# A fused attention, feed-forward and gating layer: normalized tokens transposed by VectorE and through DRAM in place of TensorE

## The chip, the cores and the metric

The kernel runs on one core of one Trainium2 chip. The time is that of the device in microseconds, from the first to the last instruction of one execution; three runs of the kernel before were timed. The profile is of one execution of its own.

## What is computed

x is [8, 2048, 512] in fp32: 8 batches of 2048 tokens. Cut to what matters:

```python
xn = layernorm(x)                          # over the 512 channels
q = xn @ Wq.T + bq                         # 8 heads of 8 channels
k = xn @ Wk.T + bk                         # 8 heads of 8 channels
v = xn @ Wv.T + bv                         # 8 heads of 64 channels
scores = leaky_relu(q k^T / sqrt(8), 0.2)  # 2048 x 2048 for each head and batch
s = gamma * (softmax(scores) @ v) + xn
g = silu(xn @ W.T + gated low-rank experts(xn))   # gate: softmax over 4, top 1
out = x + s * g
```

## The kernel before

**Tiles and stages.** A batch is cut into NB = 4 blocks of 512 tokens (BLK), a block into NT = 4 tiles of 128 tokens; the channels are NC = 4 groups of 128. Attention runs over 16 stripes in each batch: a stripe s is one pair of heads (NPAIR = 4) and one block of 512 queries. A stripe has CH = 16 steps, one for each 128 keys. The main loop runs over all 8 x 16 stripes and 16 steps of each, 2048 steps. In each step TensorE makes the scores of the next step for two heads (`score`, L641), one unit of the row maxima of a later stripe (`max_unit`, L586), and subtracts the maxima from this step's scores (`less_max`, L658); ScalarE does the leaky ReLU (`leaky`, L652) and the exponential (`exp`, L670); VectorE reduces the maxima (L597); GpSimd adds up the exponentials (`add_up`, L702). TensorE's products with the values (`weigh`, L682, "a value pair" for one step's two heads) wait in a list `last` until they are taken out one or two steps at a time.

**Work beside the attention.** Between these, `half_full` in each step issues a piece of background work from Python generators: `ending` (normalizes and stores a finished stripe), `shift_rows` (prepares a stripe's maxima and sends them through DRAM: L623 and L630) and `back`, the list of tasks. For each batch b the tasks are, in this order: `lift_block` 1 and 2 (gate and feed-forward of a block of batch b), `project_block` 0 and 1 of batch b + 1 (query, key and value projections), `lift_block` 3, `project_block` 2 and 3, and `lift_block` 0 of batch b + 1. Their due times come from estimated costs (A1 for a projection, A2 for a lift) spread over stripes 1.3 to 13.8 of the batch (`due_at`); a task may run ahead by AHEAD = 6 units. `spend` counts what was done. A generator's yield tells what comes next: HOLD (in the midst of matmuls into one PSUM bank), WAIT (the next piece waits for another engine), TINY (a short piece of TensorE), FREE, SLOW, IDLE. `half_full` has four branches:

```python
if go_on():                      # a generator in WAIT went on
    values(run); return
if state[j] == TINY:             # one value pair and the short piece
    values(min(run, 1)); go(j); ended[0] = True
elif len(last) > MUCH - (state[j] != HOLD) or (ended[0] and run > 1):
    for g in stats.values(): next(g, None)   # one piece of norm
    values(run)                  # value pairs
else:
    go(j); ...                   # matmuls of a task, two if in HOLD
```

**The place of the change.** While the task before a `project_block` runs, `norm` of its block is advanced in the third branch: statistics of four tiles on VectorE (L304, L305), their power on GpSimd, the first tile's normalization on ScalarE (L319, from tile xt into tile xn). `project_block` runs what is left of `norm`, then transposes each 128-token tile by four TensorE matmuls with the identity (L370, into PSUM tile tp), normalizes the next one meanwhile, and copies the result on VectorE (L373) to xnT, which holds channels on partitions and 512 tokens in the free dimension. Then it loads x for the block after the next (`load_x`, L111), projects queries and keys (`project`, L265, rhs xnT), splits them (`split_keys`, eight stores to KS and QS, L338 and L343), stores xn to XN (L389) and xnT to XT (L390) in DRAM, and projects the values (`token_major`, L279, lhsT xnT). `lift_block` reads xnT back from XT (`fetch`, L328). All DMAs are issued by SyncE's queue (SP), in program order; an issue that has to wait holds up those behind it. `load_stacks` (L542 k, L548 q_sb) loads a stripe's keys and queries at the start of the second stripe before it; the maxima of that stripe begin six steps later. Batch 0 is normalized and transposed ahead of the loop by code of its own (`turn`, L932), with nothing to hide it.

A token's place: a block's token p * 4 + t lies on partition p in tile t (`(n p t)`). Attention sums over all keys, so any order serves as long as queries, outputs, x and XN agree.

Of the kernel before, what the change touches and what calls it, by code (L numbers as in the profile page):

```python
# [20 lines left out]
BLK = 512  # L21
# [11 lines left out]
def fused_layer_kernel(  # L33
# [44 lines left out]
    xv = x.rearrange("b (n p t) c -> b n p t c", p=128, t=NT)  # L78
    ov = out.rearrange("b (n p t) c -> b n p t c", p=128, t=NT)
# [18 lines left out]
    XN = [tc.dram_tile([NB, 128, NT, C], FP, name=f"XN{b}") for b in range(B)]  # L98
    XT = [tc.dram_tile([NB, 128, NC, BLK], FP, name=f"XT{b}") for b in range(B)]

# [4 lines left out]
    def load_x(b, n):  # L105
        xt = two.tile([128, NT, C], FP, name="xt")
        if (b, n) == (0, 0):
            for t in range(NT):
                nc.sync.dma_start(out=xt[:, t, :], in_=xv[b, n][:, t, :])
        else:  # L110
            nc.sync.dma_start(out=xt, in_=xv[b, n])  # L111
        xtiles[b, n] = xt
# [136 lines left out]
    def spend(cost):  # L249
        spent[0] += cost  # L250
# [8 lines left out]

    def project(ps, wt, xnT):  # L260
        for c in range(NC):
            for part in pieces():
                if c or part.start:
                    yield HOLD
                nc.tensor.matmul(  # L265
                    ps[:, part],
                    lhsT=wt[:, c, :],
                    rhs=xnT[c][:, part],
                    start=(c == 0 and part.start == 0),
                    stop=(c == NC - 1 and part.stop == BLK),  # L270
                )
                spend(MM / len(pieces()))

    def token_major(ps, wt, xnT, t, more=False):
        for c in range(NC):
            for part in pieces():
                if c or part.start:
# [3 lines left out]
                    lhsT=xnT[c][:, t * 128 : (t + 1) * 128],  # L281
# [6 lines left out]
    def columns(*tiles):  # L288
        return [a[:, c, :] for a in tiles for c in range(a.shape[1])]
# [8 lines left out]
    def norm(b, n):  # L298
# [17 lines left out]
        xn = two.tile([128, NT, C], FP, name="xn")  # L316

        def normalize(t):
            nc.scalar.activation(  # L319
                xn[:, t, :], xt[:, t, :], AF.Identity, bias=nmr[:, t : t + 1], scale=rstd[:, t : t + 1]  # L320
            )

        normalize(0)
        normed[b, n] = xn, normalize
# [36 lines left out]
    def project_block(b, n, prefetch):  # L361
# [3 lines left out]
        xn, normalize = normed.pop((b, n))  # L365
        xnT = two.tile([128, NC, BLK], FP, name="xnT")
        for t in range(NT):
            tp = bank([128, NC, 128], "tp")
            for c in range(NC):
                nc.tensor.transpose(tp[:, c, :], xn[:, t, c * 128 : (c + 1) * 128], ident)  # L370
            if t + 1 < NT:
                normalize(t + 1)
            nc.vector.tensor_copy(xnT[:, :, t * 128 : (t + 1) * 128], tp)  # L373
            spend(0.5)
            yield TINY if t + 1 < NT else FREE
        if prefetch:
            fetch(*prefetch)
        nxt = b * NB + n + 2
        if nxt < B * NB:
            load_x(nxt // NB, nxt % NB)  # L380

        ps = bank([128, BLK], "qkps")
        yield from project(ps, wqk_sb, columns(xnT))
# [5 lines left out]
        nc.sync.dma_start(out=XN[b][n], in_=xn)  # L389
        nc.sync.dma_start(out=XT[b][n], in_=xnT)  # L390
# [5 lines left out]
        for t in range(NT):  # L396
            ps = bank([128, C], "vps")
            yield from token_major(ps, wv_sb, columns(xnT), t)
# [6 lines left out]
    def lift_block(b, n, prefetch, cols=None):  # L405
# [3 lines left out]
        if not early:  # L409
            if (b, n) not in fetched:  # L410
                fetch(b, n)
            cols = columns(fetched.pop((b, n)))
# [293 lines left out]
    def read_for_ending(s):  # L706
# [9 lines left out]
        nc.sync.dma_start(out=xs[:, 1], in_=XN[b][n][:, :, cols])  # L716
# [49 lines left out]
    A1, A2, LIFTED, KEYED, VALUED = 20 * MM + 2.0, 24 * MM + 3.7, 1.3, 13.8, 15.0  # L766
# [79 lines left out]

    def half_full():
# [8 lines left out]
        if go_on():  # L856
            values(run)
            return
# [3 lines left out]
        if j is not None and state[j] == TINY:  # L862
            values(min(run, 1))
            go(j)
            ended[0] = True
        elif j is None or len(last) > MUCH - (state[j] != HOLD) or (ended[0] and run > 1):
            ended[0] = False
            for g in stats.values():
                next(g, None)
# [32 lines left out]
    with tc.manual_schedule():  # L902
# [5 lines left out]
        def normalize_all(own, n):  # L908
# [5 lines left out]
            nc.sync.dma_start(out=XN[0][n], in_=xn)  # L914
# [208 lines left out]
```

## Time and profile before

| | us |
|---|---|
| median of three runs | 5573.27 (5553.82 to 5576.89) |
| span of the profiled execution | 5580.8, 78283 instructions |
| TensorE (PE) busy | 5338.6, 96% |
| GpSimd (POOL) busy | 4778.5, 86% |
| ScalarE (ACT) busy | 4448.0, 80% |
| VectorE (DVE) busy | 3672.4, 66% |
| mean granted TensorE clock | 0.970 |
| DMA | 615.39 MB, 35.1% of 16 engines on SP's queue |

The profiled execution's own time is its span, from its first to its last instruction; nothing else is told of it. Busy is the time in which an engine works on an instruction; matmuls are pipelined and their ends modelled, so a busy TensorE is not at its peak. PEld is TensorE's weight load, which runs beside the matmuls. An fp32 matmul shows as two rows. A name such as `tp<-ident,xn` is the tile written and the tiles read, L370 the line of the kernel. What stands behind `<-` after a time is what ended the wait; a wait for several events is put down to the last. The granted clock is the share of full rate at which TensorE ran.

### The profile page before, as it was taken

The numbers are of one execution on the slowest core, as the hardware profiler recorded it, in microseconds if no ns is written. First come the engines' busy times: TensorE is split into PE (matmuls) and PEld (weight loads), VectorE is DVE, ScalarE is ACT, GpSimd is POOL, SyncE is SP. The second block draws the span as 40 slices with busy tenths as digits, with TensorE's granted clock in tenths as the row PEclk, the third lists the DMA queues.
The fourth block names the chain that finished last, engine by engine and source line by source line (L and its number), as shares of the span: only waits on it lengthen the run. The fifth ranks groups of instructions, "written<-read, shape, count | busy, mean of one in ns | idle before, by whom it ended". The sixth has DMA issues, their size and how long they took to land.

```text
span 5580.8 us, 78283 instructions
## 1 busy us (share of the span) xinstructions
PE 5338.6 (96%) x26258; PEld 1975.0 (35%) x26258; DVE 3672.4 (66%) x4990; ACT 4448.0 (80%) x8627; POOL 4778.5 (86%) x2906
## 2 busy tenths in 40 slices
PE   7999999999999999999999999999999999999998
PEld 3333333333333333333333333333333333333332
DVE  5665766667666666667667666676666667666663
ACT  1787888788887788878888788887788878888887
POOL 1887898889897889988899888898889988899898
PEclk9998999999998999999999999999999999999998
DMA  5333343334423343333432334323343242432221
GB/s 191 113 111 114 109 133 97 101 116 120 125 94 95 124 127 111 98 101 124 136 108 88 108 116 152 101 80 117 111 146 95 83 144 88 142 96 84 72 78 61
DMA packets 528265, 615.39 MB, mean 110 GB/s; under 512 B 44092, under 2 KB 438332, under 8 KB 491768
## 3 DMA queue, kind: packets, MB, share of 16 engines
q1 hardware_dynamic: 527864, 610.39, 35.1%
q8 instruction: 209, 3.42, 0.3%
q14 instruction: 192, 1.57, 0.1%
HBM read 407.88 MB, written 202.38 MB: 109 GB/s over the span
## 4 chain that ended last, share of the span: by engine, by line
PE 84%; ACT 8%; DMA 3%; DVE 2%; issue 1%; SPq 1%; POOL 0%; ACTq 0%; POOLq 0%; DVEq 0%
PE av L682 30%; PE sc L658 17%; PE zps L279 9%; PE vps L279 8%; PE mx L586 8%; ACT ex L670 5%; ACT sc L652 3%; DMA q_sb<-QS 2%; PE qkps L265 2%; PE pps L265 2%; PE dps L265 2%; PE atp L754 1%; PE dps L737 1%; PE tp L370 1%; DVE mxr L597 1%
## 5 line engine op out<-in xcount | busy, mean ns | idle before, releaser
L702 POOL TENSOR_TENSOR acc<-acc,ex 128x1024 f32<-128x1024 f32 x1792 | 4231.4, 2361 | 255.3 <-ACT ex L670 138.4
L597 DVE TENSOR_REDUCE mxr<-mx 128x2 f32<-128x1024 f32 x2030 | 2480.0, 1222 | 1209.7 <-PE sc L658 942.8
L670 ACT ACTIVATE ex<-sc 128x512 f32<-128x512 f32 x4096 | 2228.5, 596 | 951.8 <-PE sc L658 831.3
L652 ACT ACTIVATE sc<-sc 128x512 f32<-128x512 f32 x4096 | 2234.4, 591 | 17.9 <-PE sc L641 17.9
L682 PE MATMUL av<-ex,v_sb 128*64 128x512 f32 x8192 | 2140.3, 627 | 4.5 <-DVE avs L724 3.1
L658 PE MATMUL sc<-shift,ones_r 2*128 2x512 f32 x4096 | 1654.7, 462 | 77.7 <-ACT sc L652 65.8
L586 PE MATMUL mx<-k,q_sb 32*128 32x512 f32 x4096 | 1463.2, 453 | 66.3 <-DMA q_sb<-QS 62.4
L658 PEld LDWEIGHTS sc<-shift,ones_r 2*128 2x128 f32 x4096 | 694.8, 187 | 1542.3 <-ACT sc L652 1453.1
L641 PE MATMUL sc<-q_sb,k 32*128 32x512 f32 x4096 | 1036.4, 502 | 0.0
L682 PEld LDWEIGHTS av<-ex,v_sb 128*64 128x64 f32 x8192 | 468.6, 138 | 843.1 <-issue 819.5
L586 PEld LDWEIGHTS mx<-k,q_sb 32*128 32x128 f32 x4096 | 572.6, 187 | 90.5 <-issue 69.8
L279 PE MATMUL zps<-w_sb,xnT 128*128 128x512 f32 (+1 forms) x1120 | 529.0, 589 | 7.5 <-DMA xnT<-XT 7.5
L279 PE MATMUL vps<-wv_sb,xnT 128*128 128x512 f32 x960 | 477.1, 621 | 0.2
L702 POOL TENSOR_TENSOR acc<-ex 128x1024 f32<-128x1024 f32 x128 | 301.8, 2357 | 169.0 <-ACT ex L670 168.7
L641 PEld LDWEIGHTS sc<-q_sb,k 32*128 32x128 f32 x4096 | 385.4, 185 | 0.8 <-issue 0.8
L279 PEld LDWEIGHTS zps<-w_sb,xnT 128*128 128x128 f32 x1120 | 187.0, 190 | 234.9 <-issue 229.7
L279 PEld LDWEIGHTS vps<-wv_sb,xnT 128*128 128x128 f32 x960 | 164.5, 190 | 200.1 <-issue 198.7
L518 DVE SCALAR_TENSOR_TENSOR g<-th,zps 128x512 f32<-128x512 f32 x128 | 88.0, 688 | 185.0 <-ACT th L517 185.0
L611 POOL TENSOR_TENSOR ml<-m,big 128x8 f32<-128x8 f32 x128 | 26.2, 205 | 202.5 <-DVE m L610 196.3
L349 DVE TENSOR_TENSOR vb<-vps,bv_sb 128x512 f32<-128x512 f32 x120 | 82.9, 691 | 93.4 <-PE vps L279 93.2
L373 DVE COPY xnT<-tp 128x512 f32<-128x512 f32 x112 | 77.3, 690 | 97.5 <-PE tp L370 97.5
L265 PE MATMUL dps<-xnT,wd_sb 128*128 128x512 f32 (+1 forms) x280 | 134.4, 592 | 0.0
(124 smaller groups left out, 2717.7 us busy)
## 6 DMA issues: line engine op xcount, KB each, us to landing
v_sb<-VS SPq DMA_DIRECT2D x127, 1024.0 KB
k<-KS SPq DMA_DIRECT2D x256, 256.0 KB
XN<-xn SPq DMA_DIRECT2D x32, 1024.0 KB
q_sb<-QS SPq DMA_DIRECT2D x256, 128.0 KB
xnT<-XT SPq DMA_DIRECT2D x32, 1024.0 KB
GS<-g SPq DMA_DIRECT2D x32, 1024.0 KB
gs<-GS SPq DMA_DIRECT2D x128, 256.0 KB
xs<-in_x_dram SPq DMA_DIRECT2D x128, 256.0 KB
```

The lines of the kernel that those rows point to most:

```text
L265: nc.tensor.matmul(ps[:, part], lhsT=wt[:, c, :], rhs=xnT[c][:, part], start=(c == 0 and part.start == 0), stop=(c == NC - 1 and part.stop ...
L279: nc.tensor.matmul(ps[:, part], lhsT=xnT[c][:, t * 128 : (t + 1) * 128], rhs=wt[:, c, part], start=(c == 0 and part.start == 0), stop=(c = ...
L349: nc.vector.tensor_tensor(vb[:, :, t, :], ps.rearrange("p (h d) -> p h d", h=NPAIR), bv_sb.rearrange("p (h d) -> p h d", h=NPAIR), ALU.add,)
L518: nc.vector.scalar_tensor_tensor(g[:, t, :], th, 1.0, ps, ALU.add, ALU.mult)
L586: nc.tensor.matmul(parts[e], lhsT=q_sb[r, t * 128 : (t + 1) * 128], rhs=k_sb[r, kb // 2 * BLK : (kb // 2 + 1) * BLK], start=True, stop=True,)
L597: nc.vector.reduce_max(mxr[s][:, :, t, kb : kb + 1], mx, axis=AX.X)
L641: nc.tensor.matmul(sc[e], lhsT=k_sb[r, i // 2 * 128 : (i // 2 + 1) * 128], rhs=q_sb[r, :], start=True, stop=True,)
L652: nc.scalar.activation(sc[e], sc[e], AF.Prelu, alpha=SLOPE)
L658: nc.tensor.matmul(sc[e], lhsT=ones_r[r, :], rhs=shifts[s][r, :], start=False, stop=True, skip_group_check=True,)
L670: nc.scalar.activation(ex[:, e, :], sc[e], AF.Exp, scale=qscale)
L682: nc.tensor.matmul(avt[s][64 * e : 64 * e + DV, :], lhsT=v_sb[:, i, 64 * e : 64 * e + DV], rhs=ex[:, e, :], start=(i == 0), stop=(i == CH ...
L702: nc.gpsimd.tensor_tensor(acc[s], old, ex, ALU.add)
```

## The change

For batches 1 to 7, `norm` does more than it did. It normalizes in place (xt), transposes each tile on VectorE in 32x32 blocks into tile xb, and writes the pieces to XT by four DMAs, each from 32 partitions, so that in DRAM the blocks come to stand where a whole transpose would have them; it writes xn to XN by four DMAs, loads x for the block after the next by four DMAs, and fetches xnT from XT for `project_block`, which no longer transposes. The columns of xnT are now in four runs of 128 for each channel group (`turned_columns`), so the rhs of a projection is read with a stride. Tokens lie in natural order (`(n t p)`). `prepare` advances `norm` in the first two branches of `half_full` too. The stores of XN and XT after the key split are gone. xt moves to a pool of three buffers, the pool of two for xn goes, xb has one. A1 loses the 2.0 of the transposes. Batch 0 keeps TensorE's transposes; its xn is in place, too.

```diff
--- before.py
+++ after.py
@@ -75,8 +75,9 @@
     CH = NB * NT
     SEQ = NPAIR * NB
 
-    xv = x.rearrange("b (n p t) c -> b n p t c", p=128, t=NT)
-    ov = out.rearrange("b (n p t) c -> b n p t c", p=128, t=NT)
+    xv = x.rearrange("b (n t p) c -> b n p t c", p=128, t=NT)
+    ov = out.rearrange("b (n t p) c -> b n p t c", p=128, t=NT)
+    xq = x.rearrange("b (n a t i) c -> b n a i t c", a=4, t=NT, i=32)
     qscale = 1.0 / (DQK ** 0.5)
 
     const = ctx.enter_context(tc.tile_pool(name="const", bufs=1))
@@ -95,20 +96,22 @@
     KS = [tc.dram_tile([HEADS, 4, DQK, M], FP, name=f"KS{b}") for b in range(B)]
     VS = [tc.dram_tile([NPAIR, 128, CH, 128], FP, name=f"VS{b}") for b in range(B)]
     GS = [tc.dram_tile([NB, 128, NT, C], FP, name=f"GS{b}") for b in range(B)]
-    XN = [tc.dram_tile([NB, 128, NT, C], FP, name=f"XN{b}") for b in range(B)]
+    XN = [tc.dram_tile([NB, BLK, C], FP, name=f"XN{b}") for b in range(B)]
     XT = [tc.dram_tile([NB, 128, NC, BLK], FP, name=f"XT{b}") for b in range(B)]
+    XTQ = [xt_b.rearrange("n (f j) c m -> n f j (c m)", f=4) for xt_b in XT]
 
     SH = [tc.dram_tile([2, 2, NT, 4, 32], FP, name=f"SH{i}") for i in range(2)]
 
     xtiles = {}
 
     def load_x(b, n):
-        xt = two.tile([128, NT, C], FP, name="xt")
+        xt = qp.tile([128, NT, C], FP, name="xt")
         if (b, n) == (0, 0):
             for t in range(NT):
                 nc.sync.dma_start(out=xt[:, t, :], in_=xv[b, n][:, t, :])
         else:
-            nc.sync.dma_start(out=xt, in_=xv[b, n])
+            for t in range(NT):
+                nc.sync.dma_start(out=xt[:, t, :], in_=xq[b, n][:, :, t, :] if b else xv[b, n][:, t, :])
         xtiles[b, n] = xt
 
     load_x(0, 0)
@@ -257,6 +260,10 @@
             return [slice(0, BLK // 2), slice(BLK // 2, BLK)]
         return [slice(0, BLK)]
 
+    def tokens(cols, part):
+
+        return cols[:, part.start // 128 : part.stop // 128]
+
     def project(ps, wt, xnT):
         for c in range(NC):
             for part in pieces():
@@ -265,7 +272,7 @@
                 nc.tensor.matmul(
                     ps[:, part],
                     lhsT=wt[:, c, :],
-                    rhs=xnT[c][:, part],
+                    rhs=tokens(xnT[c], part),
                     start=(c == 0 and part.start == 0),
                     stop=(c == NC - 1 and part.stop == BLK),
                 )
@@ -278,7 +285,7 @@
                     yield HOLD
                 nc.tensor.matmul(
                     ps[:, part],
-                    lhsT=xnT[c][:, t * 128 : (t + 1) * 128],
+                    lhsT=xnT[c][:, t],
                     rhs=wt[:, c, part],
                     start=(c == 0 and part.start == 0),
                     stop=(c == NC - 1 and part.stop == BLK and not more),
@@ -286,7 +293,13 @@
                 spend(MM / len(pieces()))
 
     def columns(*tiles):
-        return [a[:, c, :] for a in tiles for c in range(a.shape[1])]
+        return [a[:, c, :].rearrange("p (t m) -> p t m", t=NT) for a in tiles for c in range(a.shape[1])]
+
+    def turned_columns(xnT):
+
+        flat = xnT.rearrange("p c m -> p (c m)")
+        by_c = flat.rearrange("p (a c m) -> p c a m", a=NT, c=NC)
+        return [by_c[:, c] for c in range(NC)]
 
     normed = {}
     stats = {}
@@ -313,15 +326,38 @@
         nc.gpsimd.tensor_tensor(nmr, nmr, minus_one.to_broadcast([128, NT]), ALU.mult)
         for _ in range(3):
             yield
-        xn = two.tile([128, NT, C], FP, name="xn")
-
         def normalize(t):
             nc.scalar.activation(
-                xn[:, t, :], xt[:, t, :], AF.Identity, bias=nmr[:, t : t + 1], scale=rstd[:, t : t + 1]
+                xt[:, t, :], xt[:, t, :], AF.Identity, bias=nmr[:, t : t + 1], scale=rstd[:, t : t + 1]
             )
 
         normalize(0)
-        normed[b, n] = xn, normalize
+        if b == 0:
+            normed[b, n] = xt, normalize
+            return
+        xb = one.tile([128, 4, NC, NT, 32], FP, name="xb")
+        for t in range(NT):
+            yield
+            nc.vector.transpose(
+                xb[:, :, :, t, :].rearrange("p f c i -> p c f i"),
+                xt[:, t, :].rearrange("p (c f j) -> p c f j", c=NC, f=4),
+            )
+            if t + 1 < NT:
+                normalize(t + 1)
+        for t in range(NT):
+            nc.sync.dma_start(
+                out=XN[b][n].rearrange("(a t i) c -> t a i c", a=4, t=NT)[t], in_=xt[:, t, :]
+            )
+        for a in range(4):
+            nc.sync.dma_start(
+                out=XTQ[b][n].rearrange("f j (a r) -> a j f r", a=4)[a],
+                in_=xb[32 * a : 32 * a + 32].rearrange("j f c t i -> j f (c t i)"),
+            )
+        nxt = b * NB + n + 2
+        if nxt < B * NB:
+            load_x(nxt // NB, nxt % NB)
+        yield
+        fetch(b, n)
 
     def fetch(b, n):
         xnT = two.tile([128, NC, BLK], FP, name="xnT")
@@ -362,32 +398,17 @@
 
         for _ in stats.pop((b, n)):
             pass
-        xn, normalize = normed.pop((b, n))
-        xnT = two.tile([128, NC, BLK], FP, name="xnT")
-        for t in range(NT):
-            tp = bank([128, NC, 128], "tp")
-            for c in range(NC):
-                nc.tensor.transpose(tp[:, c, :], xn[:, t, c * 128 : (c + 1) * 128], ident)
-            if t + 1 < NT:
-                normalize(t + 1)
-            nc.vector.tensor_copy(xnT[:, :, t * 128 : (t + 1) * 128], tp)
-            spend(0.5)
-            yield TINY if t + 1 < NT else FREE
+        cols = turned_columns(fetched.pop((b, n)))
         if prefetch:
             fetch(*prefetch)
-        nxt = b * NB + n + 2
-        if nxt < B * NB:
-            load_x(nxt // NB, nxt % NB)
 
         ps = bank([128, BLK], "qkps")
-        yield from project(ps, wqk_sb, columns(xnT))
+        yield from project(ps, wqk_sb, cols)
         nc.scalar.activation(ps, ps, AF.Identity, bias=bqk_sb)
         yield WAIT
         hi = one.tile([128, BLK], FP, name="hi")
         lo = one.tile([128, BLK], FP, name="lo")
         split_keys(b, n, ps, hi, lo)
-        nc.sync.dma_start(out=XN[b][n], in_=xn)
-        nc.sync.dma_start(out=XT[b][n], in_=xnT)
         if n == NB - 1:
             ready.append(b)
         yield FREE
@@ -395,7 +416,7 @@
         vb = one.tile([128, NPAIR, NT, 128], FP, name="vb")
         for t in range(NT):
             ps = bank([128, C], "vps")
-            yield from token_major(ps, wv_sb, columns(xnT), t)
+            yield from token_major(ps, wv_sb, cols, t)
             add_bias(vb, t, ps)
             yield FREE if prefetch or t + 1 < NT else TINY
         store_values(b, n, vb)
@@ -409,7 +430,8 @@
         if not early:
             if (b, n) not in fetched:
                 fetch(b, n)
-            cols = columns(fetched.pop((b, n)))
+            xnT = fetched.pop((b, n))
+            cols = turned_columns(xnT) if b else columns(xnT)
             if prefetch:
                 fetch(*prefetch)
 
@@ -713,7 +735,7 @@
         nc.sync.dma_start(out=gs, in_=GS[b][n][:, :, cols])
         xs = two.tile([128, 2, NT, 128], FP, name="xs")
         nc.sync.dma_start(out=xs[:, 0], in_=xv[b, n][:, :, cols])
-        nc.sync.dma_start(out=xs[:, 1], in_=XN[b][n][:, :, cols])
+        nc.sync.dma_start(out=xs[:, 1], in_=XN[b][n].rearrange("(t p) c -> p t c", p=128)[:, :, cols])
         reads[s] = gs, xs
 
     def ending(s):
@@ -763,7 +785,7 @@
         nc.sync.dma_start(out=ov[b, n][:, :, cols], in_=gs)
 
 
-    A1, A2, LIFTED, KEYED, VALUED = 20 * MM + 2.0, 24 * MM + 3.7, 1.3, 13.8, 15.0
+    A1, A2, LIFTED, KEYED, VALUED = 20 * MM, 24 * MM + 3.7, 1.3, 13.8, 15.0
     LAST = 13.5
     tasks = [(lift_block, 0, 0, 16 * MM + 1.7, LIFTED)]
     for b in range(B):
@@ -844,6 +866,10 @@
             weigh(*w)
         del last[:count]
 
+    def prepare():
+        for g in stats.values():
+            next(g, None)
+
     def half_full():
 
 
@@ -855,6 +881,7 @@
         alone = run and last[0][1] == CH - 1
         if go_on():
             values(run)
+            prepare()
             return
         j = (ahead() or [None])[0]
         if j == 2 and state[2] != HOLD and spent[0] > due[0] + AHEAD:
@@ -862,11 +889,11 @@
         if j is not None and state[j] == TINY:
             values(min(run, 1))
             go(j)
+            prepare()
             ended[0] = True
         elif j is None or len(last) > MUCH - (state[j] != HOLD) or (ended[0] and run > 1):
             ended[0] = False
-            for g in stats.values():
-                next(g, None)
+            prepare()
             values(run)
         else:
             if alone:
@@ -911,7 +938,7 @@
             xn, normalize = normed[0, n]
             for t in range(1, NT):
                 normalize(t)
-            nc.sync.dma_start(out=XN[0][n], in_=xn)
+            nc.sync.dma_start(out=XN[0][n].rearrange("(t p) c -> p t c", p=128), in_=xn)
 
         def turn(n, own, between):
```

## The prediction

> **What bounds the kernel now.** I read the page's busy times and chain first, then the waits, the groups of instructions, and the timeline around single places. A "step" below is one pass of the inner loop (one key chunk of one stripe), cut in the timeline at the first score matmul (L641); 16 steps are a stripe, 16 stripes a batch, 2048 steps the loop.
>
> ```profile
> PE 5338.6 (96%) x26258; PEld 1975.0 (35%) x26258; DVE 3672.4 (66%) x4990; ACT 4448.0 (80%) x8627; POOL 4778.5 (86%) x2906
> ...
> PE 84%; ACT 8%; DMA 3%; DVE 2%; issue 1%; SPq 1%; POOL 0%; ACTq 0%; POOLq 0%; DVEq 0%
> ```
>
> TensorE sets the end: 96% busy, 84% of the chain. Its idle time is 5580.8 - 5338.6 = 242 us, and two waits (columns: us in total, times, longest) make up 109 of it:
>
> ```profile
> PE mx L586 <- DMA q_sb<-QS: 62.4, 18, 7.3
> ...
> PE tp L370 <- ACT xn L319: 47.0, 28, 1.7
> ```
>
> The second is the place that the change removes. All 28 projected blocks of batches 1 to 7 begin with it. In the timeline of TensorE (start, us):
>
> ```profile
> 4797.58 0.49 PE L641 MATMUL sc<-q_sb,k 32*128 32x512 f32 x2
> ...
> 4801.00 0.65 PE L370 MATMUL tp<-ident,xn 128*128 128x128 f32 x4 [1.68 <-ACT xn L319]
> ...
> 4801.59 0.50 PE L641 MATMUL sc<-q_sb,k 32*128 32x512 f32 x2
> ...
> 4805.28 0.60 PE L641 MATMUL sc<-q_sb,k 32*128 32x512 f32 x2
> ```
>
> TensorE stands 1.68 us for the normalization, the step takes 4.01 us and the next 3.69. The same stop can cost more than itself. The block that starts at 460.30 us is followed by these stretches (after the engines: granted clock, DMA share, GB/s):
>
> ```profile
> 460.00:474.00 14.00, 13.70 (x50) 5.59 (x52) 6.87 (x9) 8.57 (x16) 8.02 (x4) 0.51 0.31 113
> 474.00:488.00 14.00, 13.88 (x84) 4.61 (x80) 10.79 (x16) 11.58 (x23) 11.15 (x11) 1.00 0.01 3
> ```
>
> At clock 0.51 TensorE did 50 matmuls in 14 us, at 1.00 it did 84. A half-rate stretch of 3.4 to 13.7 us begins within 2 us of 15 of the 28 starts.
>
> I then sorted the steps by what TensorE does in them besides scores and maxima. Two value pairs (8 rows of L682): 618 steps, median 2.54 us. One pair alone: 199, median 2.22, mean 2.28. One pair and four transposes (tp): 112, median 2.67, mean 3.10, 347.0 us in all. Two fp32 matmuls of a projection: 2.58. The 2.22 is ScalarE's: its four 128x512 passes (L652, L670) stand in the timeline as 2 x 1.09 us.
>
> The prices of single operations:
>
> ```profile
> L319 ACT ACTIVATE xn<-xt,nmr,rstd 128x512 f32<-128x512 f32 x128 | 101.1, 827 | 12.0 <-POOL nmr L313 9.5 <-DMA QS<-ex 2.4
> ...
> L370 PE MATMUL tp<-ident,xn 128*128 128x128 f32 x448 | 81.8, 311 | 47.0 <-ACT xn L319 47.0
> L373 DVE COPY xnT<-tp 128x512 f32<-128x512 f32 x112 | 77.3, 690 | 97.5 <-PE tp L370 97.5
> ...
> L621 DVE STREAM_TRANSPOSE cT<-c 128x32 f32<-128x32 f32 x128 | 25.7, 201 | 1.0 <-POOL c L616 1.0
> ```
>
> **What goes: transposes.** 448 L370 and 112 L373 go. The 112 pairs of value matmuls in those steps stay and need steps of their own, so a tp step becomes a one-pair step: 112 x (2.67 - 2.22) = 50 us.
>
> **What goes: the stop at each start.** 347.0 - 112 x 2.67 = 48 us of the tp steps lie above their median (stop and slow clock), and the other steps within six of a start lie 26 us above theirs: 74 us. The Trainium skill (TensorE: Matmul & The Clock Gate, "Why this matters for your kernels") puts the limit at idle gaps above about 3 us. By it a gap of 1.68 us would leave the clock alone, and the slow stretches would have another cause and stay; by it the sum would be 26 us poorer. The clock rows above show the stretches right behind the starts, and I keep the 26.
>
> **What moves: the stores of XN and XT.** They stood in the DMA queue between the key and query stores and the next stripe's loads (SP's issues; start, us of issuing):
>
> ```profile
> 1095.38 0.46 SPq L389 DMA_DIRECT2D XN<-xn  x1
> 1095.88 1.08 SPq L390 DMA_DIRECT2D XT<-xnT  x1
> 1097.06 3.06 SPq L542 DMA_DIRECT2D k<-KS  x2
> 1100.17 2.63 SPq L548 DMA_DIRECT2D q_sb<-QS  x2
> ```
>
> q_sb was issued behind 2 MB of stores, landed at 1109.0, and TensorE idled 6.3 us in a step of 10.9 us. This returns in every batch at stripe 6, step 6, and weaker at stripes 8 and 12, behind the XN and XT of the next blocks. Above their medians these steps and the three after them cost 82 + 18 + 14 = 114 us over seven batches. The eight KS and QS stores (1 MB, 5.5 us of issuing) stay in front, so I count two thirds: 75 us. Bounds: 0 and 114.
>
> **What is added on ScalarE.** The same 112 normalizations of 0.827 us, now one in a step. ScalarE has 2.18 us of work in a step, so one fits into 2.54 with 0.46 us of lag that the next step without one takes up; three or four in a row, as in lift steps, fall behind by 1.3 us. Two blocks of each batch normalize in such runs, two between projection matmuls (0.3 each): 7 x (2 x 1.3 + 2 x 0.3) = 22, say 25 us. Bounds: 0, and 112 x 0.82 = 92.
>
> **What is added on VectorE.** 112 transposes of 128x512. Nearest row: L621, 201 ns at 32 columns; PSUM copies of 64 and 128 columns take 217 and 278 ns, so a column costs 0.95 ns, and 201 + 480 x 0.95 = 0.66 us. At the other end stands 16 times L621, 3.2 us. I take 0.70, nearest to the short end and to the L373 copy it replaces (690 ns): 78 us for 77. VectorE's 34% idle hides it; where an ending's two products share the step (1.23 + 2 x 0.69 + 0.70 = 3.3 us) the maximum's reduce is late by some 0.5 us, 28 times: 14 us. The Trainium skill (VectorE: DVE Perf Modes, "Rules for kernel authors") advises TensorE for a 128x128 transpose whose target may be PSUM, so it speaks against the change. By its table (311 ns for 128x128 in bf16, blocks only) four would take 1.24 us as an estimate, which the gaps of VectorE still hold; here TensorE is the full engine.
>
> **What is added on the queue.** Per block: 4 stores of XN, 4 of XT, 4 loads of x in place of 1, 1 and 1, and a fetch: ten more issues at 0.6 us, 6 us of SP's time, and 1 MB more. The fetch must wait for the XT stores to land, and behind it in SP's order stand the shift rows' DMAs (L623, L630), the stripe's k and q_sb and the output stores. The preparation starts with the task before its block (in a batch of before at stripe 3 step 5, 5/5, 9/1 and 11/2) and by the calls counted below stores 14 steps later in a lift task, some 18 later in a project task; starts shift a few steps at most: near 4/4, 6/9, 10/0 and 12/5. The first and last are far from the loads at a stripe's start; the second sits on the shift rows, the third on the loads. The weak events (8 and 12) cost 2.6 and 2.0 us with 2 MB in front, so I take 2 events of 2.1 us in 7 batches: 30 us. Bounds: 0, and four of the strong kind, 7 x 4 x 11.8 = 330. Strided rhs columns cost nothing: L737 reads its rhs in runs of 32 elements, its eight rows in 0.64 us.
>
> **Is the fetch in time?** The new preparation needs 12 calls (4 statistics, 3 empty ones, the first normalization, 4 transposes, the fetch; the stores come with the 11th). prepare is called in every step but those that issue projection matmuls on their own. From the start at 1059.95 to that at 1147.21 are 29 steps: 4 with tp, 10 with projection matmuls, 15 others. So at least 15 calls in 25 steps remain. The due times give a project task 17.2 of 3 x 24.3 + 4 x 17.2 - 13.8 = 128 units for 12.5 stripes, 27 steps with 17 calls; after the 11th, 6.7 to 9 steps are left, 17 to 23 us. Needed: 8 issues (4.8 us), about 3 us to land, the fetch behind the x loads about 6 us: 14 us. I take 0 for the wait.
>
> **Sum.** -50 - 74 - 75 + 25 + 14 + 30 = -130 us. The profiled execution's span is 5580.8 us, 7.5 above the median of the runs, 5573.27. 5580.8 - 130 - 7.5 = 5443 us.
>
> **Rivals.**
> Late columns (slower). If fewer than 11 calls fall into a project task before the next one, as they would with three matmul steps for each other one, the rest runs at the start of that block, and TensorE waits for the trip through DRAM: 4 x 0.70 of transposes, 4.8 of issuing, 3 to land, 6 to 10.7 to fetch (10.7 is the one fetch that the chain of before shows, at 144.44 us), 18 us, and 2 of slow clock after. It strikes the two blocks of each batch that follow a project task: 14 x 20 = 280, 5723 us. Against it: the 15 steps counted. A fetch only 3 us late would cost 14 x 6 = 84 and give 5527.
> The queue pays it back. Two bursts in each batch act like stripe 6 of before: 7 x 2 x 11.8 = 165 instead of 30, 5578 us, no change. For it: SP is in order and now waits for a landing; against it: 2 MB right ahead of the loads cost only 2.0 to 2.6 us.
> Only TensorE's own part. The key and query stores alone keep the q_sb waits: 5443 + 75 = 5518.
> Dear transposes. At 3.2 us, VectorE needs 4.4 us in a step of 2.5: 112 x 1.9 = 210, 5653 us.
>
> **How the numbers follow.** Forecast (5374 to 5500) 0.50; only TensorE's part, or a slightly late fetch (5500 to 5545) 0.20; below 5374 0.03; the queue pays it back 0.09; late columns 0.13; dear transposes 0.05. About 0.5%, 28 us, is what a measurement here can tell from no change, so faster (below 5545) is 0.73, same 0.09, slower 0.18. Low end: all 114 us of q_sb waits gone and no burst cost, 5580.8 - 50 - 74 - 114 + 25 + 14 - 7.5 = 5374. High end: 5580, which takes in the queue case and leaves out the two slower ones.
>
> **What would show it.** Right: no L370, a stream transpose of 128x512 near 0.7 us, no TensorE wait on xn, a q_sb wait well under 62 us, TensorE's matmuls fewer by 448, fewer half-rate stretches. Wrong: qkps waiting for xnT<-XT (late columns), L586 or L658 waiting for q_sb or shift in places where they did not (queue), mxr late behind a long transpose.

## The result, and the profile after

The changed kernel takes 5998.2 us (median of four runs, 5989.17 to 6007.61), the kernel before, run beside it, 5575.08: ratio 1.073, 95% interval 1.0685 to 1.0783. It is slower by 7%; the forecast was 5443 us, and the upper end of its range 5580. The profiled execution has a span of 6005.8 us, 425 more than before, and a mean granted clock of 0.926 (0.970 before).

The busy times and the chain of the changed kernel's page, one line of each:

```profile
PE 5415.4 (90%) x25810; PEld 1974.2 (33%) x25810; DVE 3658.2 (61%) x4990; ACT 4444.7 (74%) x8627; POOL 4782.0 (80%) x2906
...
PE 74%; ACT 8%; DMA 6%; SPq 5%; DVE 4%; issue 1%; POOL 0%; ACTq 0%; POOLq 0%; DVEq 0%
```

TensorE has its 448 matmuls fewer, and stands idle for 6005.8 - 5415.4 = 590 us, against 242. DMA and SP's queue hold 11% of the chain, against 4%. Of TensorE's waits (us in total, times, longest), these are the two large ones on transfers:

```profile
PE qkps L272 <- DMA xnT<-XT: 190.7, 13, 26.5
...
PE mx L608 <- DMA q_sb<-QS: 185.3, 18, 17.6
```

The wait of tp on xn is gone, but a projection now waits for its columns up to 26.5 us at a time, and the wait on q_sb, which was to shrink from 62.4 us, is 185.3. I sorted the steps again as in the prediction and took the median of its kind from each step; what is left I call excess. 6/13 below is step 13 of stripe 6. The excess of the main loop is 724 us, against 268 before. Over seven batches: 208 at step 1 of stripe 7 (xnT), 126 and 120 in stripes 4 and 10, nearly all of it around step 6 (q_sb), 38 in stripe 13 (q_sb), 32 in stripe 12 (xnT). Stripe 6, the place of the old q_sb wait, fell from 83 to 7.

One of the seven places at stripe 7, in the timeline of SP's issues (start, us that the issuing took):

```profile
1199.53 3.27 SPq L348 DMA_DIRECT2D XN<-xt  x4
1202.90 8.51 SPq L352 DMA_DIRECT2D XT<-xb  x4
1211.45 6.27 SPq L114 DMA_DIRECT2D xt<-in_x_dram  x4
1217.77 2.77 SPq L735 DMA_DIRECT2D gs<-GS  x1
1220.58 2.58 SPq L737 DMA_DIRECT2D xs<-in_x_dram  x1
1223.20 2.78 SPq L738 DMA_DIRECT2D xs<-XN  x1
1226.34 0.94 SPq L364 DMA_DIRECT2D xnT<-XT  x1
```

and the wait that it makes, in the timeline of TensorE, with two windows of it (after the engines' busy times: granted clock, DMA share, GB/s):

```profile
1237.74 2.07 PE L272 MATMUL qkps<-xnT,wqk_sb 128*128 128x512 f32 x2 [26.53 <-DMA xnT<-XT]
```

```profile
1212.00:1218.00 6.00, 0.00 (x0) 0.00 (x0) 0.00 (x0) 0.00 (x0) 0.00 (x0) 0.62 0.51 158
1218.00:1227.00 9.00, 0.00 (x0) 0.00 (x0) 0.00 (x0) 0.00 (x0) 0.00 (x0) 0.50 0.45 143
```

From the first store's issue to the fetch's are 26.8 us, to the matmul 38.2. All engines stand, the clock falls to half, and the DMA engines that everybody waits for are half idle. The DMA view of the second window, in 40 slices (tenths of 16 engines, then GB/s), shows how:

```profile
DMA  2222222222222223589984222554999622222246
GB/s 91 100 100 100 100 100 109 100 100 109 100 100 100 100 109 114 155 234 294 348 250 125 73 109 91 105 105 150 305 348 319 180 64 91 100 91 98 93 146 207
```

The floor is a quarter, about 100 GB/s: as much as 4 of the 16 engines make. It is what is left of the XN stores and x loads. Each of their DMAs takes one tile t, and its DRAM side is "a i c": the outermost dimension is a, of size 4. The Trainium skill (DMA: Bandwidth & Descriptors, "Rules for kernel authors") says that an outermost dimension of size c < 16 confines the whole DMA to at most c engines. The row agrees with it. Only where a gs or xs read gets through do the slices reach 9. SP's issues of these three reads take 2.6 to 2.8 us each; in experiment 1 below, without the four-engine transfers, they take 0.5 to 0.6.

### The profile page after: what moved, and what is told of

It reads as the page before. It is cut to its first block, busy times and chain, and to the rows that moved or that the text cites. A ratio compares the mean times of both kernels' runs of the same rounds, so it can differ in the third digit from the quotient of the medians.

```text
span 6005.8 us, 77588 instructions
## 1 busy us (share of the span) xinstructions
PE 5415.4 (90%) x25810; PEld 1974.2 (33%) x25810; DVE 3658.2 (61%) x4990; ACT 4444.7 (74%) x8627; POOL 4782.0 (80%) x2906
## 4 chain that ended last, share of the span: by engine, by line
PE 74%; ACT 8%; DMA 6%; SPq 5%; DVE 4%; issue 1%; POOL 0%; ACTq 0%; POOLq 0%; DVEq 0%
PE av L704 26%; PE sc L680 15%; PE zps L286 8%; PE vps L286 7%; PE mx L608 7%; ACT ex L692 5%; DMA xnT<-XT 3%; ACT sc L674 2%; PE qkps L272 2%; PE pps L272 2%; PE dps L272 2%; DMA q_sb<-QS 2%; DVE mxr L619 1%; SPq L570 1%; SPq L352 1%
## 5 line engine op out<-in xcount | busy, mean ns | idle before, releaser
L704 PE MATMUL av<-ex,v_sb 128*64 128x512 f32 x8192 | 2178.5, 637 | 7.2 <-DVE avs L746 4.0
L680 PE MATMUL sc<-shift,ones_r 2*128 2x512 f32 x4096 | 1691.5, 471 | 129.1 <-ACT sc L674 122.7
L608 PE MATMUL mx<-k,q_sb 32*128 32x512 f32 x4096 | 1483.8, 462 | 202.6 <-DMA q_sb<-QS 185.3
L680 PEld LDWEIGHTS sc<-shift,ones_r 2*128 2x128 f32 x4096 | 712.0, 190 | 1722.2 <-ACT sc L674 1576.8
L663 PE MATMUL sc<-q_sb,k 32*128 32x512 f32 x4096 | 1054.2, 511 | 0.0
L286 PE MATMUL zps<-w_sb,xnT 128*128 128x512 f32 (+1 forms) x1120 | 548.1, 607 | 25.9 <-DMA xnT<-XT 25.9
L272 PE MATMUL qkps<-xnT,wqk_sb 128*128 128x512 f32 x240 | 160.8, 784 | 192.9 <-DMA xnT<-XT 190.7
L272 PEld LDWEIGHTS qkps<-xnT,wqk_sb 128*128 128x128 f32 x240 | 47.6, 231 | 266.4 <-DMA xnT<-XT 202.1
```

The costliest lines, as they stand in the source:

```text
L272: nc.tensor.matmul(ps[:, part], lhsT=wt[:, c, :], rhs=tokens(xnT[c], part), start=(c == 0 and part.start == 0), stop=(c == NC - 1 and part ...
L286: nc.tensor.matmul(ps[:, part], lhsT=xnT[c][:, t], rhs=wt[:, c, part], start=(c == 0 and part.start == 0), stop=(c == NC - 1 and part.stop ...
L608: nc.tensor.matmul(parts[e], lhsT=q_sb[r, t * 128 : (t + 1) * 128], rhs=k_sb[r, kb // 2 * BLK : (kb // 2 + 1) * BLK], start=True, stop=True,)
L663: nc.tensor.matmul(sc[e], lhsT=k_sb[r, i // 2 * 128 : (i // 2 + 1) * 128], rhs=q_sb[r, :], start=True, stop=True,)
L680: nc.tensor.matmul(sc[e], lhsT=ones_r[r, :], rhs=shifts[s][r, :], start=False, stop=True, skip_group_check=True,)
L704: nc.tensor.matmul(avt[s][64 * e : 64 * e + DV, :], lhsT=v_sb[:, i, 64 * e : 64 * e + DV], rhs=ex[:, e, :], start=(i == 0), stop=(i == CH ...
```

## Experiments

Ratios are to the kernel before, run on the same chip, with a 95% interval. The edits are shortened: (..) and words such as "XT stores" stand for longer code.

**1 to 3. Sixteen engines in place of four.** The same bytes, four DMAs each, cut by partitions (a outside, 32 rows of i outermost) and not by tile.

```diff
-dma_start(out=xt[:, t, :], in_=xq[b, n][:, :, t, :])                # x loads
+dma_start(out=xt[32*t : 32*t+32], in_=xq[b, n][t])
-dma_start(out=XN(.. "t a i c")[t], in_=xt[:, t, :])                 # XN stores
+dma_start(out=XN(.. "a i t c")[a], in_=xt[32*a : 32*a+32])
```

> Edit: the four stores of XN and the four loads of x of a block are cut by quarters of the partitions (32 partitions with all four tiles each) and not by tiles; the same bytes, the same 2 KB runs, the same number of DMAs; only the outermost dimension of the DRAM side becomes 32 in place of 4. Theory A (a DMA whose DRAM side begins with a dimension of 4 runs on 4 of the 16 DMA engines, about 100 GB/s, and everything queued later waits for these four): the xnT wait of 190.7 us falls under 30 us, the q_sb wait of 185.3 us under 50 us, and the time from 5998 us to 5450 to 5580. Theory B (SP's order: the fetch waits for a landing and holds up the loads behind it, and the preparation is ready too late in a project task, whatever the speed of the DMAs): each of the two waits keeps over half of its size, and the time stays above 5800 us.

> Edit: only the four loads of x are cut by quarters of the partitions; the stores of XN stay as in the changed kernel. Theory A: 1 MB on four engines is left (10 us), ahead of the XT stores; the wait for xnT at stripe 7 of a batch (about 26 us) falls by about 10 us, and the time lies between that of the changed kernel and that of the run with both, 5650 to 5850 us. Theory B: little changes, over 5900 us.

> Edit: only the four stores of XN are cut by quarters of the partitions; the loads of x stay. Theory A: the XT stores land early, but the x loads, 10 us on four engines, still stand ahead of the fetch and of the k and q_sb loads: 5650 to 5850 us, with the gain against the changed kernel about half of that of the run with both. Theory B: over 5900 us.

Both (e1_spread): 5693.14 us, 1.0175 (1.0119 to 1.0230). Loads alone: 5778.26, 1.0339 (1.0288 to 1.0390). Stores alone: 5924.55, 1.0597 (1.0539 to 1.0655). From 1.0734 the loads take off 4.0 points, the stores 1.4, both 5.6: the two parts add up within the intervals, and three quarters of the loss was the shape of two access patterns. Theory A had the cause, not all of the sizes. With both, the wait on q_sb falls to 44.0 us as expected, that on xnT only to 73.0, and the time stays above its range. The loads alone came as expected; the stores alone gained a quarter, not half, of what both gain, and stayed above 5900. The loads weigh more at both waits: with them xnT falls from 190.7 to 119.9 us and q_sb from 185.3 to 66.2, with the stores to 155.0 and 126.7. They stand last in the burst, right ahead of what is waited for; that this makes the difference was not tested alone. The same place with both cut so, in SP's timeline and in the DMA view from 1140 to 1152 us:

```profile
1139.52 3.34 SPq L351 DMA_DIRECT2D XN<-xt  x4
1142.96 4.56 SPq L355 DMA_DIRECT2D XT<-xb  x4
1147.56 2.50 SPq L115 DMA_DIRECT2D xt<-in_x_dram  x4
...
1151.92 0.50 SPq L367 DMA_DIRECT2D xnT<-XT  x1
```

```profile
DMA  8999999899979999999987999987799778999969
GB/s 251 294 292 283 232 212 198 171 205 205 171 171 348 294 273 232 178 191 287 335 294 246 280 266 259 300 273 266 232 239 212 150 205 253 341 300 171 205 171 198
```

The fetch is issued 12.4 us after the first store, not 26.8, and the sixteen engines are busy for six tenths or more of every slice, nine in most. What is left of the wait on xnT is one stop of some 10 us in each batch:

```profile
PE qkps L275 <- DMA xnT<-XT: 73.0, 7, 11.3
```

**4. Another order, with the four engines kept.** XT stores and fetch first, then XN stores and x loads.

```diff
-XN stores; XT stores; x loads; empty call; fetch
+XT stores; empty call; fetch; XN stores; x loads
```

> Edit: the XT stores first, then the fetch, and behind it the XN stores and the x loads; all DMAs in the form of the changed kernel (four engines for XN and x). Theory A: nothing on four engines stands ahead of the fetch, so the wait for xnT falls under 30 us, but 20 us of work on four engines still stands ahead of the next k and q_sb loads or beside them: the q_sb wait stays above 100 us; 5650 to 5850 us. Theory B: the fetch still waits for the XT stores to land and holds up what is behind it; the wait for xnT stays above 90 us and the time above 5850 us.

6100.65 us, 1.0906 (1.0854 to 1.0959): slower than the changed kernel. Both waits came as theory A expected, but its time, 5850 at most, did not. The waits:

```profile
PE mx L608 <- DMA q_sb<-QS: 276.3, 21, 28.4
...
PE mx L608 <- DMA KS<-lo: 74.7, 6, 15.9
PE sc L680 <- DMA shift<-SH: 69.8, 8, 10.7
...
PE qkps L272 <- DMA xnT<-XT: 19.5, 7, 7.6
```

The wait on xnT nearly goes, so the fetch was late because of what stood ahead of it. But the slow transfers then stand ahead of every other load, and cost more there. The transfers take some 20 us for a block (an estimate: 2 MB at the 100 GB/s above), and moving them in the queue here only chose who waits for them.

**5. Without the added calls.** e1_spread, with the preparation in the third branch of `half_full` only.

```diff
 if go_on():
     values(run)
-    prepare()
 ...
     go(j)
-    prepare()
```

> Base as before (all 16 engines). Edit: undoes one part of the change: the preparation advances in the third branch of the step alone, as in the kernel before, so at most starts of a block much of it is left and is run there at once. Theory: then the prediction's rival of late columns holds at all 28 starts: 28 stops of 12 to 18 us and slow clock after, 350 to 600 us over the base's 5693: 6050 to 6300 us. If the calls do not matter (the trip through DRAM is what counts): within 50 us of the base.

6134.05 us, 1.0987 (1.0942 to 1.1032). The columns are late at all 28 starts:

```profile
PE qkps L275 <- DMA xnT<-XT: 589.4, 28, 23.8
```

This is the price of the rival "late columns" at full strength: some 21 us for each block, near the 18 that it had worked out. The added calls are needed for the trip through DRAM.

**6. The trip earlier.** e1_spread, statistics of two tiles in one call, one empty call fewer, XT stores ahead of XN stores: the fetch comes with the ninth call, not the twelfth.

```diff
-if t + 1 < NT: yield          # statistics
+if t == 1: yield
-for _ in range(3): yield
+for _ in range(2): yield
-XN stores; XT stores; x loads; empty call; fetch
+XT stores; XN stores; x loads; empty call; fetch
```

> Base: the run with XN and x cut by quarters of the partitions (all 16 engines). Edit: the XT stores go ahead of the XN stores, and the preparation needs 9 calls in place of 12 (statistics of two tiles in a call, two empty calls for three). Theory A2 (what is left of the wait for xnT, 73 us, comes from the burst beginning only four or five steps before the block that needs it): the wait falls under 20 us and the time by 60 to 120 us, to 5570 to 5640; the q_sb wait near stripe 4 may move or go. Theory B2 (the rest is the trip through DRAM itself, whose queue is full at that place whenever it starts): the wait stays above 50 us and the time within 30 us of the base's 5693.

5634.77 us, 1.0097 (1.0070 to 1.0124). No projection of batches 1 to 7 waits for xnT. What remained were two waits on loads at the start of a stripe:

```profile
PE mx L611 <- DMA q_sb<-QS: 52.6, 8, 7.2
...
PE sc L683 <- DMA shift<-SH: 45.6, 17, 5.2
```

The first lies nearly all at step 6 of stripe 12, 8.6 us of excess in each batch; the second, on the shift rows, at the first steps of stripes 4, 7 and 10. At stripe 12 the burst lies right ahead of the loads (SP's timeline):

```profile
1352.63 2.87 SPq L351 DMA_DIRECT2D XT<-xb  x4
1355.59 4.25 SPq L356 DMA_DIRECT2D XN<-xt  x4
1359.89 2.91 SPq L115 DMA_DIRECT2D xt<-in_x_dram  x4
1362.84 0.43 SPq L367 DMA_DIRECT2D xnT<-XT  x1
1363.37 1.58 SPq L567 DMA_DIRECT2D k<-KS  x2
1365.00 1.85 SPq L573 DMA_DIRECT2D q_sb<-QS  x2
```

**7. The burst in two halves.** e5_early, in which the XN stores and x loads, 2 of the 4 MB, move behind the second value tile of the block.

```diff
 # norm: XT stores; empty call; fetch
-XN stores; x loads
 # project_block
 add_bias(vb, t, ps)
+if t == 1: XN stores; x loads
```

> e5_early (5634.77) with the XN stores and the loads of the next x, 2 MB of the 4 MB that its norm issues at once, put behind the second value tile of the same block. The transposes stay on VectorE and go through DRAM. Theory A (what is left of the loss in e5 is the bytes of a block's burst standing ahead of q_sb, where the burst falls at the first steps of a stripe, as at step 6 of stripe 12, 8.6 us in each batch): the wait on q_sb falls from 52.6 to under 20 us, the wait on xnT stays under 5, the time is 5545 to 5590. Rival B (it is the 2 MB of the XT round trip itself, with its pieces of 32 partitions, that the loads stand behind): q_sb stays at 35 to 55 us, and the time is 5605 to 5640. Rival C (x arrives too late for the next block's norm): the wait on xnT comes back, over 30 us, and the time is above 5640.

5527.78 us, 0.9892 (0.9849 to 0.9936): theory A, and better than its figure. The wait on the shift rows is back at 5.3 us, too. VectorE's transposes and the trip through DRAM are now faster than the kernel before. The same place, and the wait:

```profile
1331.09 3.15 SPq L351 DMA_DIRECT2D XT<-xb  x4
1338.50 0.34 SPq L361 DMA_DIRECT2D xnT<-XT  x1
1338.94 1.38 SPq L573 DMA_DIRECT2D k<-KS  x2
1340.37 1.32 SPq L579 DMA_DIRECT2D q_sb<-QS  x2
```

```profile
PE mx L617 <- DMA q_sb<-QS: 11.2, 8, 2.2
```

**8. The stores alone.** The kernel before, with nothing changed but the place of its XN and XT stores.

```diff
 split_keys(b, n, ps, hi, lo)
-dma_start(out=XN[b][n], in_=xn); dma_start(out=XT[b][n], in_=xnT)
 ...
 add_bias(vb, t, ps)
+if t == 1: dma_start(out=XN[b][n], in_=xn); dma_start(out=XT[b][n], in_=xnT)
```

> The kernel before with one edit: the stores of XN and XT of a projected block stand after its second value tile, not between the key split and the next stripe's loads. It measures the prediction's moved term alone. If the q_sb waits (62.4 us, and 114 us with the slow clock) come from these 2 MB: the q_sb wait under 25 us, 5575 - 75 to -114, 5460 to 5510 us. If the eight key and query stores and SP's own wait for the split make it: the q_sb wait stays above 40 us and the time above 5540 us.

5505.99 us, 0.9857 (0.9817 to 0.9898). Two moved lines give 68 us of span. The waits that the prediction started from:

```profile
PE tp L370 <- ACT xn L319: 47.0, 28, 1.7
...
PE mx L587 <- DMA q_sb<-QS: 5.0, 4, 2.0
```

The first is as before, the second was 62.4.

**9. What a kernel without transposes could win.** The kernel before without the transposes and copies of batches 1 to 7; the columns are read from batch 0's blocks in DRAM, so the trip of a block's own columns is left out and the output is built from batch 0's tokens. The normalizations stand beside the value projection, and the XN stores and x loads behind it.

> The kernel before with the TensorE transposes of batches 1 to 7 and VectorE's copies left out: project_block takes an xnT read from DRAM, of the same block of batch 0, issued when its preparation begins, so nothing waits for it, and its output is built from those tokens. The normalizations run beside the value projection, XN is stored and x is loaded after it, A1 has the change's value. It measures the prize alone: the prediction's 50 us of transposes and 74 us of stops. If that accounting holds: 5575 - 124, 5430 to 5480 us, no wait for xn. If ScalarE's normalizations are what the transposes' steps really cost, and they now cost the same in other steps: 5520 to 5570 us.

5500.45 us, 0.9851 (0.9804 to 0.9899). It gains 75 us in this form, between its two expectations. Most of the prize that the prediction saw is in it: the medians of its steps sum to 32 us less, and the excess at the four starts falls by 70. But the time does not measure that alone. With the XN stores elsewhere, stripe 6 loses 70 us of excess and stripe 13 gains 52, with most of the 35.4 us of waits on q_sb that remain. The gain is also no more than the moved stores give by themselves (experiment 8).

**10. Only the normalizations ahead of the block.** e9_later_stores, and all four normalizations of a block in `norm`'s own calls, advanced as in the changed kernel. TensorE transposes.

```diff
 normalize(0)
+if b:
+    for t in range(1, NT): yield; normalize(t)
 ...
-if t + 1 < NT: normalize(t + 1)           # project_block
 if go_on():
-    values(run); return
+    values(run); prepare(); return         # also behind go(j) in the TINY branch
```

> The kernel before with two edits that need no trip through DRAM: its XN and XT stores moved behind the second value tile (as in e9_later_stores, 5505.99 us, VectorE's and TensorE's shares as before), and the preparation of the changed kernel, which takes up to nine calls a block and has all four normalizations done when the block's transposes start. TensorE still transposes. Theory A (the stop of about 1.68 us at the start of 28 blocks and the half clock behind it were worth what the prediction put on them, 48 + 26 us, and they come from the normalizations that follow one tile at a time, not from the transposes): the waits of the tp transposes on xn fall from 47.0 to under 8 us, the excess at the block starts (about 100 us in e9) falls by 50 to 80, the time is 5425 to 5460. Rival B (ScalarE's normalizations in four calls in a row hold up as many exponentials as the stop cost; the changed kernel shows 0.6 to 1.6 us of excess in each step of such a run): the wait falls too, the excess moves to the steps before the block start, and the time is 5480 to 5530. Rival C (the half clock does not follow from the stop): the wait falls by 40 us and nothing else, 5465 to 5480.

5470.34 us, 0.9781 (0.9744 to 0.9818), the fastest of all, with the granted clock at 0.981. Against e9_later_stores the ratios differ by 0.8%, 42 us; their intervals just touch. By its time it lies between theory A and rival B, where rival C stood; the steps show that A and B are both in it. The tp matmuls of this kernel, with what they waited for (the view of one tile):

```profile
L374 PE MATMUL tp<-ident,xn x448: 272/273/333, 369.6 to 4674.5; 128*128 128x128 f32 x150
L940 PE MATMUL tp<-ident,xn x64: 272/273/476, 11.2 to 52.6; 128*128 128x128 f32 x64
its engine sat idle before it (us, times) until:
  ACT xn L319: 11.2, 1
  DVE ex L339: 5.7, 2
  DVE scale_sb L195: 0.3, 1
```

All three waits belong to the opening (L940); the 28 later starts have none. The excess at the starts (five steps each from 5/5, 7/2, 11/2 and 12/15) falls from 83 to 13 us, a tp step's median from 2.67 to 2.45 us. In return the excess of stripes 3, 4, 9 and 10, where blocks are prepared, grows from 24 to 64 us: 22 of it from 4/0 to 4/6 and from 9/11 to 10/3, where normalizations stand in a row, 14 from 3/8 to 3/15, where the same calls now bunch the statistics. Stretches at half the clock in the main loop, but for the one at its start, go from 32 (259 us) to 23 (172 us). The starts lose 23 us more than the stop alone, which rival C didn't allow.

Beside e11_early_apart, which prepares as early but transposes on VectorE: the medians of all steps sum to 5164 us here and 5161 there, the excess is 164 here and 220 there. So once its steps hold no normalization, TensorE's transposing costs no more in the medians than the other way, and the 56 us of excess between the two decide. The two kernels also bunch their statistics differently, so not all of that need be the trip.

**11. Normalizations on VectorE.** The same, with one VectorE multiply and add in place of each ScalarE pass.

> e10_norm_ahead (0.9781 of the kernel before) with the normalizations of batches 1 to 7 on VectorE, one multiply and add of 128x512 each, at the same places, in place of ScalarE's. It tells whether the excess that is left in the steps with normalizations in a row (in e10 about 0.4 to 0.9 us each, some 25 us over the seven batches at steps 0 to 3 of stripe 4 and from step 14 of stripe 9 to step 3 of stripe 10) belongs to ScalarE, whose exponentials they hold up. Theory A (it does): that excess goes, nothing takes its place, and the ratio is 0.972 to 0.976. Rival B (VectorE's maxima are as tight: its statistics, at about 0.68 us each, show excess of 0.6 to 0.7 us too, at steps 9, 11 and 12 of stripe 3): the excess stays at the same steps within a third, and the ratio is 0.977 to 0.981. Rival C (VectorE is tighter than ScalarE): the excess grows, above 0.981.

5520.89 us, 0.9880 (0.9856 to 0.9905): rival C. One operation takes 1.200 us (groups of instructions, of this kernel and of e10_norm_ahead):

```profile
L320 DVE TENSOR_SCALAR xn<-xt,rstd,nmr 128x512 f32<-128x512 f32 x112 | 134.4, 1200 | 0.0
```

```profile
L319 ACT ACTIVATE xn<-xt,nmr,rstd 128x512 f32<-128x512 f32 x128 | 105.7, 835 | 12.4 <-POOL nmr L313 12.4
```

The excess at steps 0 to 6 of stripe 4 grows from 13 to 50 us, and at steps 10 to 13 of stripe 11, the other large place, from 8 to 48. There TensorE's maxima matmuls wait for VectorE's reduction. In all, by the waits of e10_norm_ahead and then of this kernel:

```profile
PE mx L589 <- DVE mxr L600: 10.6, 36, 0.6
```

```profile
PE mx L594 <- DVE mxr L605: 55.7, 70, 2.2
```

VectorE is busy for two thirds of the span (68%), but its maxima come in every step, and 1.20 us beside their 1.22 makes 2.42 in steps of 2.2 to 2.5 us. Its idle share was no cover.

## Why the prediction was wrong

**The step that failed: the price of the queue.** "Needed: 8 issues (4.8 us), about 3 us to land, the fetch behind the x loads about 6 us: 14 us. I take 0 for the wait." The 0.6 us for an issue and the landing came from DMAs of before that run on 16 engines. The four-DMA forms of the XN stores and x loads run at a quarter of that width, some 20 us for the 2 MB of a block, and issues behind them take up to 2.8 us. At the place shown, 38.2 us were needed. The diff of the change shows it (`xq[b, n][:, :, t, :]`, `"t a i c"`); the prediction counted how many DMAs there were and how many bytes, not how wide each is. Experiments 1 to 3 show this cause: with the width alone put right, 5.6 of the 7.3 points go.

**The time that was left.** "6.7 to 9 steps are left, 17 to 23 us." At the place shown the stores were issued at 6/13, and the block starts at 7/1: four steps, 11 us. The stores came near the places foretold (4/0, 6/13, 9/12 and 12/5 for 4/4, 6/9, 10/0 and 12/5); a difference of four steps at 6/13 was the margin. So even 14 us would have been late there, and e1_spread, at 16 engines, still loses 10 us at this block. The rival "late columns" had the right wait and sign, but its condition, too few calls, did not hold: the calls came, the transfers were slow.

**Term of the queue, +30.** It measured 284 us: excess of 126, 120 and 38 in stripes 4, 10 and 13, up to 17.6 us for one wait. The bound of 330 held it, but was worked out from bursts on 16 engines. "The queue pays it back" counted two events a batch of 11.8 us; there were two of 17 to 18 and a smaller third.

**Transposes, -50.** The medians of all steps together gave -29. One-pair steps rose by 78 (199 to 277), not by 112: in 29 other steps the displaced value pair joined two projection matmuls, at 2.98 us. And half of the 0.45 us by which a tp step lies above 2.22 was not TensorE's: with the normalization taken out of it, the step is at 2.45 (experiment 10). VectorE's price was right, in the groups of the changed kernel:

```profile
L341 DVE STREAM_TRANSPOSE xb<-xt 128x512 f32<-128x512 f32 x112 | 78.3, 699 | 0.0
```

**The stop and the slow clock, -74.** Right in size: experiment 10 takes 70 us from the block starts. That the clock is part of it is supported, not shown: fewer half-rate stretches follow when the 1.68 us stops go, but 23 remain and no run changed the clock alone. The rule of the Trainium skill that the prediction weighed (TensorE: Matmul & The Clock Gate, "Why this matters for your kernels") puts the limit at about 3 us, above these gaps; the sum without the 26 us would have fitted the 70 less well.

**The q_sb wait, -75.** Right in size: experiment 8 gives 68 us for it, and stripe 6 of the changed kernel lost 76 us of excess. The gain was real and was overpaid elsewhere.

**ScalarE, +25, and VectorE, +14.** Together about right: the four stripes of preparation show +42 us in e11_early_apart, where no transfer hides it, and +40 in e10_norm_ahead. But the parts were probably put wrong. The second has no VectorE transposes and pays as much, and 14 us of it lie where statistics are bunched, which the prediction did not count.

**The sum.** -130 was forecast and the span grew by 425: 555 us apart. If the other terms are taken as forecast, the queue's term accounts for 284 - 30 = 254, the fetch for 208 + 32 = 240 at the block starts of stripes 7 and 12, the transposes for 21. The first stripe and the last batch, which these sums leave out, hold 29 us more excess than before. These make 544; the 11 that are left were not traced.

## What to carry to other kernels

Read the outermost dimension of every new DMA before counting its bytes: transfers split into four by an inner index moved about 100 GB/s here, where 16 engines moved 150 to 350, and everything queued behind them paid. A burst's cost depends on what stands behind it in the queue, so place stores by the next load that is urgent, not by when their data is ready. A change that bundles several edits should be taken apart: here two moved stores and an earlier normalization, with the transposes left on TensorE, gave 2.2%, and the step that names the change, in the best form found for it, stayed 1.1 points behind that.

## What the runs showed of the hardware

Transfers whose DRAM side has an outermost dimension of 4 held about a quarter of the DMA engines' time and about 100 GB/s, while the same bytes with 32 outermost, with the reads between them, moved 150 to 350 GB/s (e1_spread, the window shown). SP's issue of one DMA grew from 0.5 to 2.8 us behind them. A VectorE multiply and add of 128x512 in fp32 with two operands per partition took 1.200 us, the 32x32 transposes of the same tile 0.699 us, ScalarE's pass 0.835 us.
